# A graph layer and an attention layer in one kernel: row sums and rows of logits taken another way

## The chip, the cores and the metric

The kernel runs on one core of one Trainium2 chip. The metric is device time of one launch in microseconds (us). TensorE does the matmuls, VectorE (DVE) and ScalarE (ACT) read their results from PSUM, GpSimd (POOL) works on SBUF alone, and SyncE (SP) issues nearly all DMAs.

## The reference, cut to what matters

There are 64 samples of 256 tokens with 512 features, all in float32, and one adjacency matrix of 256 x 256 for all of them.

```python
h = relu(layernorm(x))                                    # layer 0
Wh = h @ W;  e_src = Wh @ a_src;  e_dst = Wh @ a_dst
logits = leaky_relu(e_src[:, :, None] + e_dst[:, None, :], 0.2)
attn = softmax(where(adj == 0, -inf, logits))             # over the last axis
x = x + attn @ Wh
h = relu(layernorm(x))                                    # layer 1: 8 heads of 64
q, k, v = heads of h @ Wq.T + bq, h @ Wk.T + bk, h @ Wv.T + bv
attn = softmax(where(adj == 0, -inf, q @ k.T / 8))
x = x + concat(attn @ v) @ Wo.T + bo
```

Two things in it matter here. In layer 0 a logit is the sum of a number of the row and a number of the column. And each softmax needs its row's sum, in layer 0 one for each of 256 rows, in layer 1 one for each of 8 x 256.

## The kernel before, in words

A group g is one sample; there are G = 64. Tokens or features lie on the 128 partitions. Each stage of the work on a group is a Python generator that gives out a piece at each `yield`, and the lists `first_half` and `second_half` (L1025 to L1031) say by hand in which order the pieces of different groups follow each other. The order in which instructions are given out is the order on each engine. Iteration i works on scores of group i, on layer 0 of groups i+1 to i+3, and on the output of groups before; the second member of each pair in the lists is what is added to i. Big products are done with seven block products in place of eight (`products`, matmuls at L207 and L216), whose sums are put together by VectorE (L192 to L203, `add_to_rows` at L701) and whose operands are prepared by GpSimd (`combine`, L165 to L168). PSUM is a ring of eight banks (`bank`).

The stages that the change touches:

- `normalize0` (D0 is its last piece, at i+2). It ends with es and ed, the numbers of the rows and columns, as scalar products of h with two weight vectors: four instructions on VectorE (L511). es lies on partitions, as [128, 2].
- `weights0` (E0, at i+2, three pieces). It brings es into a row on all partitions: two transposes on TensorE (L525) into a bank `pe`. From this ScalarE makes exp of the sum and exp of 0.2 times the sum (L532, L533, four instructions), VectorE takes the maximum of the two (L537), which is exp of the leaky logit, GpSimd multiplies by the mask (em, L540) and adds the two halves (esum, L542). The third piece sums over partitions: a matmul of `ones` with esum (L556) gives the sum of each row, in all partitions at once, and VectorE makes reciprocals of it, in a tile of 128 x 256 (L558, L559).
- `quarters0` (Q0, at i+2) multiplies em by that tile on GpSimd (L578) and forms differences for the block products (eq, L588). `aggregate0` (U0 at i+2, its last piece US at i+1) does the products (L606).
- `attention` (six pieces; A at i, and A_OLD at i-1 for the last two). The pieces are the scores with their exponentials (L838, L846), four times masks and sums of two heads (L851, L853), and the values (L863, L871) with `head_sums`: eight matmuls, each in a 32-column strip of the array, give the sums of all heads (psm, L878), and VectorE the reciprocals rc (L886). Each head's row of rc is then spread over 64 partitions into rb, with eight DMAs from SBUF to SBUF (L909). `scale` (AS) multiplies by rb (L936).
- `bias_rows` (BO) adds the output bias to x on GpSimd (L929), `project_v` is V, `project_qk` is K, `output` is O, and `transform0` is W.

In the loop, groups from `PLAIN` = 3 on take the way with block products in layer 0; groups 0 to 2 take a plain one. SP issues, in this order within an iteration: the x load for group i+3 (L225), two stores of output rows (L957), and the eight rb DMAs.

Of the kernel before, what the change touches and what calls it, by code (L numbers as in the profile page):

```python
# [9 lines left out]
F32 = mybir.dt.float32  # L10
# [6 lines left out]
P = 128  # L17
# [6 lines left out]
Q = 32  # L24
# [4 lines left out]
def kernel(  # L29
# [26 lines left out]
    nc = tc.nc  # L56
    B, N, D = x.shape
    NC = N // P
    DC = D // P
    NT = GB * NC  # L60
    TOK = NT * P
    G = B // GB
    DH = D // HEADS
# [5 lines left out]
    dram = ctx.enter_context(tc.tile_pool(name="dram", bufs=1, space=bass.MemoryType.DRAM))  # L69
# [10 lines left out]
    ident = const.tile([P, P], F32, tag="ident", name="ident")  # L80
    make_identity(nc, ident)
    ones = const.tile([P, P], F32, tag="ones", name="ones")
# [49 lines left out]
    def bounded():  # L132
        weights = ctx_b.enter_context(tc.tile_pool(name="weights", bufs=1))
        big = ctx_b.enter_context(tc.tile_pool(name="big", bufs=1))
        work = ctx_b.enter_context(tc.tile_pool(name="work", bufs=1))
# [3 lines left out]
        def bank(shape, name):  # L139
            return ps_mm.tile(shape, F32, tag="mm", name=name)  # L140
# [207 lines left out]
        pick = weights.tile([P, P], F32, tag="pick", name="pick")  # L348
# [10 lines left out]
        def constants():  # L359

            ok = weights.tile([P, 2 * DC + 5], F32, tag="ok", name="ok")
            rows = weights.tile([P, 2 * DC], F32, tag="rows", name="rows")
            gms = []
            for n in range(2):
                w_q = whole((wq_sb, wk_sb)[n])  # L370

                gm = work.tile([P, DC, DH], F32, tag="gram", name=f"gram_{n}", bufs=2)
                gms.append(gm)
                for pair in range(2):
                    pg = bank([P, 2, DH], f"pgram_{n}_{pair}")
                    for e in range(2):
                        for c in range(DC):
                            for r in range(2):
                                at = e * P + r * DH
                                wc = w_q[c // 2][pair][:, c % 2, at : at + DH]  # L380
                                nc.tensor.matmul(
                                    pg[r * DH : (r + 1) * DH, e, :], wc, wc,
                                    start=(c == 0), stop=(c == DC - 1),
                                )
                    yield
                    nc.vector.tensor_copy(gm[:, 2 * pair : 2 * pair + 2, :], pg)
                    yield
            for n, gm in enumerate(gms):
                pgs = [bank([P, DC, DH], f"pgram2_{n}_{r}") for r in range(2)]
                for e in range(DC):  # L390
                    for r in range(2):
                        half_p = slice(r * DH, (r + 1) * DH)
                        part = gm[half_p, e, :]
                        nc.tensor.matmul(pgs[r][half_p, e, :], part, part, start=True, stop=True)
                yield
                for e in range(DC):
                    for r in range(2):
                        half_p = slice(r * DH, (r + 1) * DH)
                        ab = work.tile([P, DH], F32, tag="gabs", name=f"gabs_{n}_{e}_{r}")
                        nc.scalar.activation(  # L400
                            ab[half_p], pgs[r][half_p, e, :], AF.Abs,
                            accum_out=rows[half_p, n * DC + e : n * DC + e + 1],
                        )
                yield
            for _ in range(10):
                yield
            sq = weights.tile([P, 4], F32, tag="sq", name="sq")
            for j, col in enumerate((cols["bq"], cols["bk"])):
                junk = work.tile([P, DC], F32, tag="e2", name=f"junk_c_{j}")
                nc.vector.scalar_tensor_tensor(  # L410
                    junk, col, 1.0, col, op0=ALU.mult, op1=ALU.mult, accum_out=sq[:, j : j + 1]
                )
            for _ in range(4):
                yield
            pq = bank([P, 2], "pq")
            nc.tensor.matmul(pq, ones, sq[:, 0:2], start=True, stop=True)
            yield
            nc.vector.tensor_scalar(
                ok[:, 2 * DC + 2 : 2 * DC + 4], pq, 1.0, None, op0=ALU.is_le
            )  # L420
            yield
            for j in range(2):
                junk = work.tile([P, D], F32, tag="e2", name=f"junk_w_{j}")
                nc.vector.scalar_tensor_tensor(
                    junk, wa[j], 1.0, wa[j], op0=ALU.mult, op1=ALU.mult, accum_out=sq[:, 2 + j : 3 + j]
                )
                yield
            nc.vector.tensor_scalar(ok[:, 0 : 2 * DC], rows, 1.0, None, op0=ALU.is_le)
            nc.vector.tensor_scalar(ok[:, 2 * DC : 2 * DC + 2], sq[:, 2:4], 1.95, None, op0=ALU.is_le)
            yield  # L430
            big_v = weights.tile([P, 1], F32, tag="big_v", name="big_v")
            nc.vector.tensor_reduce(big_v, svs, AX.X, ALU.add)
            nc.vector.tensor_scalar(
                ok[:, 2 * DC + 4 : 2 * DC + 5], big_v, 1.0e6, None, op0=ALU.is_le
            )
            okm = weights.tile([P, 1], F32, tag="okm", name="okm")
            nc.vector.tensor_reduce(okm, ok, AX.X, ALU.min)
            for _ in range(12):
                yield
            pk = bank([1, 1], "pok")  # L440
            nc.tensor.matmul(pk, okm, ones[:, 0:1], start=True, stop=True)
            nc.vector.tensor_scalar(flag, pk, P - 0.5, None, op0=ALU.is_lt)
            yield
            picks()
            yield

        class Stats:

# [32 lines left out]
        def normalize0(g):  # L481
# [26 lines left out]
            for t in range(NT):  # L508
                for dst, a in ((es, 0), (ed, 1)):
# [3 lines left out]
                        accum_out=dst[:, t : t + 1],  # L513
                    )
            nodes[g] = h, es, ed
            yield

        def weights0(g):

            h, es, ed = nodes[g]  # L520
            edl = small.tile([P, NT], F32, tag="edl", name=f"edl_{g}")
            nc.scalar.mul(edl, ed, NEG_SLOPE)
            pe = bank([P, TOK], f"pe_{g}")
            for t in range(NT):
                nc.tensor.transpose(  # L525
                    pe[:, t * P : (t + 1) * P], es[:, t : t + 1].to_broadcast([P, P]), ident
                )

            e1 = work.tile([P, NC, N], F32, tag="e1", name=f"e1_{g}")
            e2 = work.tile([P, NC, N], F32, tag="e2", name=f"e2_{g}")  # L530
# [10 lines left out]
            esum = work.tile([P, N], F32, tag="esum", name=f"esum_{g}")  # L541
            engine.tensor_tensor(esum, em[:, 0, :], em[:, 1, :], op=ALU.add)  # L542
            edges[g] = [em]
            yield

            if g == 0:
                ps = bank([P, NT], f"ps_{g}")
# [11 lines left out]
            nc.vector.reciprocal(rs, rs)  # L559
            edges[g].append(rs)  # L560
            yield


        PLAIN = 3

        def quarters0(g):

# [257 lines left out]
        def attention(g):  # L825
# [46 lines left out]

            def head_sums():

                psm = bank([P, N], f"psm_{g}")
                for r in range(2):
                    for e in range(DC):
                        nc.tensor.matmul(  # L878
                            psm[e * Q : (e + 1) * Q, :],
                            half[:, r, :],  # L880
                            sums[e][:, r, :],
                            start=(r == 0),
                            stop=(r == 1),
                        )
                rc = work.tile([P, N], F32, tag="rc", name=f"rc_{g}")
                nc.vector.reciprocal(rc, psm)  # L886
                return rc

            exs = [scores(e) for e in range(DC)]
# [13 lines left out]
                rc = head_sums()  # L903
            if g < G - 2:
                rb = work.tile([P, DC, N], F32, tag="rb", name=f"rb_{g}")
                for e in range(DC):
                    for r in range(2):
                        src = rc[e * Q + r * (Q // 2) : e * Q + r * (Q // 2) + 1, :]
                        nc.sync.dma_start(  # L909
                            rb[r * DH : (r + 1) * DH, e, :],  # L910
                            bass.AP(
                                tensor=src.tensor, offset=src.offset,
                                ap=[src.ap[0], [0, DH], [1, N]],
                            ),
                        )
            else:

                yield
                rb = [bank([P, N], f"prb_{g}_{e}") for e in range(DC)]
                for e in range(DC):  # L920
                    rows = slice(e * Q, (e + 1) * Q)
                    nc.tensor.matmul(rb[e], pick[rows, :], rc[rows, :], start=True, stop=True)
            outs[g] = aT, rb
            yield

# [89 lines left out]
        def aside(n=1):  # L1015
# [5 lines left out]
        Q0 = (quarters0, 2)  # L1021
# [1 line left out]
        A, A_OLD, BO = (attention, 0), (attention, -1), (bias_rows, 0)  # L1023
        AS, AS_OLD = (scale, -1), (scale, -2)
        first_half = [  # L1025
            (load, 3), O, D0, K, AS_OLD, O, K, O, K, E0, O, K, E0, O, US, A_OLD, K, O, K, BO, O, K, E0,
        ]
        second_half = [
            A_OLD, A, Q0, A, W, N0, W, W, V, N0, W, W, W, N1, W, N1, A, V, V, V, A, N0, N1, U0, V, AS,
            U0, X1, V, X1, V, X1,  # L1030
        ]  # L1031

# [259 lines left out]
```

## Time and profile before

| | |
|---|---|
| median of three runs | 2847.4 us (2846.96 to 2849.59) |
| the profiled execution | 2846.97 us |
| its span | 2845.2 us |
| TensorE busy | 2828.9 us (99%) |
| VectorE busy | 2473.5 us (87%) |
| GpSimd busy | 1607.0 us (56%) |
| ScalarE busy | 1257.3 us (44%) |
| TensorE clock granted | full, in the whole span |

A float32 matmul shows as two records, a transpose as one. Records of matmuls overlap, [...]so the distance between two starts says what a group costs, not its busy time. The time of an iteration is read from the distance of the same piece in two iterations. Names of tiles stand as out<-in; `pe`, `ps` and `psm` are the banks that are told of above.

### The profile page before, as it was taken

How to read it: one execution, taken by the hardware profiler on the slowest of the kernel's cores; microseconds unless marked ns; L12 is line 12 of the kernel's file. 1: busy time of each engine (PE TensorE's matmuls, PEld its weight loads, DVE VectorE, ACT ScalarE, POOL GpSimd, SP SyncE). 2: the span in 40 equal slices, each digit the busy share in tenths (PEclk: the TensorE clock that was granted, in tenths of full speed). 3: DMA queues.
4: the chain of work that ended last, by engine and by line, in shares of the span. 5: the costliest groups of instructions: out<-in, count | busy, mean ns of one | idle time of the engine just before them, and what ended most of it. 6: DMA issues, size and time to landing. Idle time of an engine off the chain costs nothing. (4 is left out here: it accounts for less than half of the span.)

```text
span 2845.2 us, 53317 instructions
## 1 busy us (share of the span) xinstructions
PE 2828.9 (99%) x20316; PEld 2472.3 (87%) x20316; DVE 2473.5 (87%) x3946; ACT 1257.3 (44%) x3045; POOL 1607.0 (56%) x2016
## 2 busy tenths in 40 slices
PE   9999999999999999999999999999999999999998
PEld 6888988988889889888898898888988988889886
DVE  7998988888889888888898888888988888889875
ACT  5444444443444444434444444344454443444532
POOL 2656556566565565665655655656556556565541
PEclk9999999999999999999999999999999999999999
DMA  4122122221221222212212222122122221221221
GB/s 134 23 38 38 34 42 33 36 45 31 38 38 34 42 33 36 45 31 38 39 33 42 33 36 46 31 38 40 32 42 33 36 45 31 38 42 30 34 42 27
DMA packets 82826, 111.01 MB, mean 39 GB/s; under 512 B 11524, under 2 KB 48644, under 8 KB 82566
## 3 DMA queue, kind: packets, MB, share of 16 engines
q1 hardware_dynamic: 82470, 107.53, 23.7%
q8 instruction: 164, 2.69, 0.4%
q14 instruction: 96, 0.79, 0.1%
q0 software_dynamic: 96, 0.01, 0.0%
HBM read 41.43 MB, written 33.55 MB: 26 GB/s over the span
## 5 line engine op out<-in xcount | busy, mean ns | idle before, releaser
L701 DVE TENSOR_TENSOR x<-po,x 128x1024 f32<-128x1024 f32 x875 | 593.8, 685 | 130.2 <-PE po L207 122.9
L851 DVE TENSOR_TENSOR ex<-ex,maskT 128x512 f32<-128x512 f32 x512 | 435.3, 890 | 0.0
L474 POOL TENSOR_SCALAR ve<-ssq 128x2 f32<-128x2 f32 x127 | 25.1, 198 | 483.8 <-ACT h L463 250.6
L846 ACT ACTIVATE ex<-psc 128x512 f32<-128x512 f32 x512 | 257.7, 627 | 89.5 <-PE psc L838 89.4
L871 ACT COPY aT<-pav 128x512 f32<-128x512 f32 x128 | 74.9, 585 | 499.2 <-PE pav L863 468.1
L511 DVE SCALAR_TENSOR_TENSOR junk<-wa,h 128x512 f32<-128x512 f32 x252 | 276.6, 1098 | 7.9 <-ACT h L504 1.1
L216 PEld LDWEIGHTS pqk<-hs,wq_sb 128*128 128x128 f32 x2016 | 264.4, 192 | 12.9
L216 PE MATMUL pqk<-hs,wk_sb 128*128 128x128 f32 x2016 | 266.3, 275 | 0.0
L216 PE MATMUL pqk<-hs,wq_sb 128*128 128x128 f32 x2016 | 265.8, 275 | 0.0
L207 PE MATMUL pv<-wv_sb,hs 128*128 128x256 f32 x1024 | 262.9, 380 | 0.6 <-DVE v L194 0.5
L540 POOL TENSOR_TENSOR em<-e,maskT 128x512 f32<-128x512 f32 x62 | 79.6, 1283 | 321.7 <-DVE e L537 312.0
L207 PE MATMUL po<-wo_sb,as 128*128 128x256 f32 x992 | 255.2, 380 | 0.0
L207 PE MATMUL po<-w_sb,us 128*128 128x256 f32 x1008 | 248.5, 379 | 0.0
L216 PEld LDWEIGHTS pqk<-hs,wk_sb 128*128 128x128 f32 x2016 | 245.4, 192 | 0.0
L838 PE MATMUL psc<-qk 64*128 64x256 f32 x2048 | 239.0, 383 | 0.3 <-DVE rc L886 0.3
L863 PE MATMUL pav<-ex,v 128*64 128x256 f32 x2048 | 235.4, 382 | 0.0
L838 PEld LDWEIGHTS psc<-qk 64*128 64x128 f32 x2048 | 193.1, 187 | 46.9 <-issue 25.0
L165 POOL TENSOR_TENSOR hs<-hT 128x256 f32<-128x256 f32 x64 | 47.0, 735 | 319.2 <-PE pv L207 319.2
L853 DVE TENSOR_TENSOR sm<-ex 128x512 f32<-128x512 f32 x256 | 210.5, 822 | 8.9
L863 PEld LDWEIGHTS pav<-ex,v 128*64 128x64 f32 x2048 | 141.2, 137 | 85.8 <-issue 20.3
L207 PEld LDWEIGHTS po<-w_sb,us 128*128 128x128 f32 x1008 | 191.4, 190 | 26.3 <-DVE x L701 0.3
L216 PEld LDWEIGHTS pqk<-hT,wq_sb 128*128 128x128 f32 x1512 | 198.2, 192 | 9.6
(211 smaller groups left out, 6564.5 us busy)
## 6 DMA issues: line engine op xcount, KB each, us to landing
x<-in_x_dram SPq DMA_DIRECT2D x64, 512.0 KB, 5.6
out_dram<-x SPq DMA_DIRECT2D x128, 256.0 KB, 2.0
rb<-rc SPq DMA_DIRECT2D x496, 64.0 KB, 4.9
wq_sb<-in_L_gnn_Wq_dram SPq DMA_DIRECT2D x4, 256.0 KB, 8.4
wk_sb<-in_L_gnn_Wk_dram SPq DMA_DIRECT2D x4, 256.0 KB, 6.7
w_sb<-in_L_gnn_W_dram SPq DMA_DIRECT2D x4, 256.0 KB, 6.6
wv_sb<-in_L_gnn_Wv_dram SPq DMA_DIRECT2D x4, 256.0 KB, 6.6
wo_sb<-in_L_gnn_Wo_dram SPq DMA_DIRECT2D x4, 256.0 KB, 6.0
```

What stands on the lines that cost most here:

```text
L165: nc.gpsimd.tensor_tensor(s[:, 0], a(1, 0), a(1, 1), op=ALU.add)
L207: nc.tensor.matmul(dst[:, 0:HD], left[:, c, :], wt[:, slot, c, :], start=c == 0, stop=c == 1)
L216: nc.tensor.matmul(dst[:, at : at + P], wt[:, slot, c, e * P : (e + 1) * P], left[:, c, :], start=c == 0, stop=c == 1,)
L511: nc.vector.scalar_tensor_tensor(junk, (wa if g else pas)[a], 1.0, h[:, t, :], op0=ALU.mult, op1=ALU.mult, accum_out=dst[:, t : t + 1],)
L540: engine.tensor_tensor(em, e1, maskT, op=ALU.mult)
L701: nc.vector.tensor_add(dst, src, dst)
L838: nc.tensor.matmul(psc[r][:, m, :], qk[rows, 2 + e % 2, m * P : (m + 1) * P], qk[rows, e % 2, :], start=True, stop=True,)
L846: nc.scalar.activation(ex[:, r, :, :], psc[r], AF.Exp, scale=SCALE)
L851: nc.vector.tensor_mul(ex[:, r, :, :], ex[:, r, :, :], maskT)
L853: nc.vector.tensor_add(sm, ex[:, :, 0, :], ex[:, :, 1, :])
L863: nc.tensor.matmul(pav[r * DH : (r + 1) * DH, i, :], v[j][:, m, at : at + DH], pair[i][:, r, m, :], start=(m == 0), stop=(m == NC - 1),)
L871: nc.scalar.copy(aT[j], pav)
```

## The change

For groups from 3 on:

1. es goes to DRAM as a row of 256 (one DMA), and comes back to all 128 partitions as `es_b` (a second DMA, in the buffer of esum). Both are issued at the end of `normalize0`. ScalarE reads `es_b` where it read the bank `pe`; the two transposes are gone.
2. The third piece of `weights0` is gone. In its place `head_sums` of group g sums the esum of group g+3 as well: four matmuls, each in a 32-column strip, each over 64 of the 256 columns, into 64 further columns of the psm bank. Maximum and reciprocal of these are on a tile of 128 x 64. The result goes to DRAM (one DMA) and comes back as `rb0` in all partitions (one DMA).
3. rc goes to DRAM in one DMA too, and rb comes back in two, in place of the eight.
4. In the order of the pieces, the first E0 stands later by one K and one O, the second E0 behind BO and A_OLD rather than ahead of US, the third is gone, and BO stands ahead of A_OLD. Near the end, one V stands ahead of both U0 rather than between them.

```diff
@@ normalize0
             nodes[g] = h, es, ed
+            if g >= PLAIN:
+                row_d = dram.tile([NT, P], F32, tag="row_d", name=f"row_d_{g}", bufs=2)
+                nc.sync.dma_start(row_d.rearrange("t p -> p t"), es)
+                es_b = work.tile([P, TOK], F32, tag="esum", name=f"es_b_{g}")
+                nc.sync.dma_start(
+                    es_b, bass.AP(tensor=row_d.tensor, offset=row_d.offset, ap=[[0, P], [1, TOK]])
+                )
+                nodes[g] = h, es_b, ed
             yield
@@ weights0
-            pe = bank([P, TOK], f"pe_{g}")
-            for t in range(NT):
-                nc.tensor.transpose(
-                    pe[:, t * P : (t + 1) * P], es[:, t : t + 1].to_broadcast([P, P]), ident
-                )
+            pe = es
+            if g < PLAIN:
+                pe = bank([P, TOK], f"pe_{g}")
...
             edges[g] = [em]
-            yield
+            if g >= PLAIN:
+                edges[g].append(esum)
+            yield
+            if g >= PLAIN:
+                return
@@ attention, head_sums
-                psm = bank([P, N], f"psm_{g}")
+                psm = bank([P, N + DH], f"psm_{g}")
+                rc = work.tile([P, N + DH], F32, tag="rc", name=f"rc_{g}")
+                g0 = g + PLAIN
+                if g0 < G:
+                    part = slice(N, N + DH)
+                    for e in range(DC):
+                        rows = slice(e * Q, (e + 1) * Q)
+                        nc.tensor.matmul(
+                            psm[rows, part], ones[:, 0:Q], edges[g0][1][:, e * DH : (e + 1) * DH],
+                            start=True, stop=True,
+                        )
...
-                rc = work.tile([P, N], F32, tag="rc", name=f"rc_{g}")
-                nc.vector.reciprocal(rc, psm)
+                if g0 < G:
+                    nc.vector.tensor_scalar_max(rc[:, part], psm[:, part], 1e-38)
+                    nc.vector.reciprocal(rc[:, part], rc[:, part])
+                    rows_d = dram.tile([P, DH], F32, tag="rows0_d", name=f"rows0_d_{g0}", bufs=2)
+                    nc.sync.dma_start(rows_d, rc[:, part])
+                    rb0 = work.tile([P, N], F32, tag="rb0", name=f"rb0_{g0}")
+                    nc.sync.dma_start(
+                        rb0.rearrange("p (e n) -> p e n", e=DC),
+                        bass.AP(
+                            tensor=rows_d.tensor, offset=rows_d.offset,
+                            ap=[[0, P], [Q * DH, DC], [1, DH]],
+                        ),
+                    )
+                    edges[g0][1] = rb0
+                nc.vector.reciprocal(rc[:, 0:N], psm[:, 0:N])
...
-                for e in range(DC):
-                    for r in range(2):
-                        src = rc[e * Q + r * (Q // 2) : e * Q + r * (Q // 2) + 1, :]
-                        nc.sync.dma_start(rb[r * DH : (r + 1) * DH, e, :], ...)
+                rows_d = dram.tile([P, N], F32, tag="rows_d", name=f"rows_d_{g}", bufs=2)
+                nc.sync.dma_start(rows_d, rc[:, 0:N])
+                for r in range(2):
+                    nc.sync.dma_start(
+                        rb[r * DH : (r + 1) * DH, :, :],
+                        bass.AP(
+                            tensor=rows_d.tensor, offset=rows_d.offset + r * (Q // 2) * N,
+                            ap=[[0, DH], [Q * N, DC], [1, N]],
+                        ),
+                    )
@@ the order
-            (load, 3), O, D0, K, AS_OLD, O, K, O, K, E0, O, K, E0, O, US, A_OLD, K, O, K, BO, O, K, E0,
+            (load, 3), O, D0, K, AS_OLD, O, K, O, K, O, K, E0, O, US, BO, A_OLD, K, E0, O, K, O, K,
...
-            A_OLD, A, Q0, A, W, N0, W, W, V, N0, W, W, W, N1, W, N1, A, V, V, V, A, N0, N1, U0, V, AS,
+            A_OLD, A, Q0, A, W, N0, W, W, V, N0, W, W, W, N1, W, N1, A, V, V, V, A, N0, N1, V, U0, AS,
             U0, X1, V, X1, V, X1,
```

A scratch tile of the checks at the start (`gabs`) moves into the buffer of rc, which is 64 columns wider.

More of the change, by code (lines that the diff above doesn't have):

```diff
@@ L398, in constants @@
                         half_p = slice(r * DH, (r + 1) * DH)
-                        ab = work.tile([P, DH], F32, tag="gabs", name=f"gabs_{n}_{e}_{r}")
+                        ab = work.tile([P, DH], F32, tag="rc", name=f"gabs_{n}_{e}_{r}")
                         nc.scalar.activation(
@@ L445, in constants @@
             yield
+        PLAIN = 3
         class Stats:
@@ L522, in weights0 @@
             nc.scalar.mul(edl, ed, NEG_SLOPE)
-            pe = bank([P, TOK], f"pe_{g}")
-            for t in range(NT):
-                nc.tensor.transpose(
-                    pe[:, t * P : (t + 1) * P], es[:, t : t + 1].to_broadcast([P, P]), ident
-                )
+            pe = es
+            if g < PLAIN:
+                pe = bank([P, TOK], f"pe_{g}")
+                for t in range(NT):
+                    nc.tensor.transpose(
+                        pe[:, t * P : (t + 1) * P], es[:, t : t + 1].to_broadcast([P, P]), ident
+                    )
             e1 = work.tile([P, NC, N], F32, tag="e1", name=f"e1_{g}")
@@ L561, in weights0 @@
             yield
-        PLAIN = 3
         def quarters0(g):
@@ L878, in head_sums @@
                         nc.tensor.matmul(
-                            psm[e * Q : (e + 1) * Q, :],
+                            psm[e * Q : (e + 1) * Q, 0:N],
                             half[:, r, :],
@@ L905, in attention @@
                 rb = work.tile([P, DC, N], F32, tag="rb", name=f"rb_{g}")
-                for e in range(DC):
-                    for r in range(2):
-                        src = rc[e * Q + r * (Q // 2) : e * Q + r * (Q // 2) + 1, :]
[L909 to L915, printed above, removed]
+                rows_d = dram.tile([P, N], F32, tag="rows_d", name=f"rows_d_{g}", bufs=2)
[7 more added lines that the diff above has]
+                        ),
+                    )
             else:
@@ L921, in attention @@
                     rows = slice(e * Q, (e + 1) * Q)
-                    nc.tensor.matmul(rb[e], pick[rows, :], rc[rows, :], start=True, stop=True)
+                    nc.tensor.matmul(rb[e], pick[rows, :], rc[rows, 0:N], start=True, stop=True)
             outs[g] = aT, rb
```

## The prediction

> **What bounds the kernel now.** I read the busy shares first, then one stretch of three samples, then TensorE's own order of time, then the waits, then the DMA issues. The page's head:
>
> ```profile
> span 2845.2 us, 53317 instructions
> PE 2828.9 (99%) x20316; PEld 2472.3 (87%) x20316; DVE 2473.5 (87%) x3946; ACT 1257.3 (44%) x3045; POOL 1607.0 (56%) x2016
> ```
>
> TensorE leaves 16 us free in the whole span. In the steady loop it leaves none: this is the table by stage (stretch, length, busy time of PE, PEld, DVE, ACT, POOL, clock, DMA share, GB/s).
>
> ```profile
> 1255.00:1386.25 131.25, 131.25 (x950) 115.76 (x949) 115.80 (x184) 58.41 (x142) 76.96 (x96) 1.00 0.24 37
> ```
>
> So one sample is 131.25 / 3 = 43.75 us of gapless TensorE work at full clock, and only two things can move the time: TensorE work taken out or put in, and a new wait of TensorE. The timeline of TensorE gives the price of what goes (start, busy time, line). First an iteration in the middle, then the one iteration near the end in which no layer 0 weights are made any more:
>
> ```profile
> 1393.65 1.06 PE L216 MATMUL pqk<-hT,wk_sb 128*128 128x128 f32 x8
> 1394.55 0.38 PE L525 MATMUL pe<-ident,es 128*128 128x128 f32 x2
> 1394.77 1.03 PE L207 MATMUL po<-wo_sb,as 128*128 128x256 f32 x4
> ...
> 1404.47 1.06 PE L216 MATMUL pqk<-hs,wk_sb 128*128 128x128 f32 x8
> 1405.37 0.60 PE L556 MATMUL ps<-esum,ones 128*128 128x256 f32 x2
> 1405.89 3.67 PE L863 MATMUL pav<-ex,v 128*64 128x256 f32 x32
> 1409.50 1.07 PE L878 MATMUL psm<-sm,half 128*32 128x256 f32 x16
> 1410.50 3.73 PE L838 MATMUL psc<-qk 64*128 64x256 f32 x32
> ```
>
> ```profile
> 2749.78 1.06 PE L216 MATMUL pqk<-hT,wk_sb 128*128 128x128 f32 x8
> 2750.67 1.03 PE L207 MATMUL po<-wo_sb,as 128*128 128x256 f32 x4
> ...
> 2760.38 1.06 PE L216 MATMUL pqk<-hs,wk_sb 128*128 128x128 f32 x8
> 2761.36 3.67 PE L863 MATMUL pav<-ex,v 128*64 128x256 f32 x32
> ```
>
> Busy times overlap, so I take differences of starts. The waits show that nobody holds TensorE up, while the other engines wait for it or for VectorE (who waited for whom, total us, times, longest):
>
> ```profile
> POOL em L540 <- DVE e L537: 312.0, 61, 7.7
> DVE rc L886 <- PE psm L878: 103.4, 63, 3.9
> PE pt L750 <- ACT xn L729: 4.9, 3, 3.1
> ```
>
> For the transfers that are added, the nearest rows (queue, count, KB, us from issue to landing), and for the added matmuls the nearest group, 64 columns wide in 64-column tiles (durations, first and last start):
>
> ```profile
> x<-in_x_dram SPq DMA_DIRECT2D x64, 512.0 KB, 5.6
> out_dram<-x SPq DMA_DIRECT2D x128, 256.0 KB, 2.0
> rb<-rc SPq DMA_DIRECT2D x496, 64.0 KB, 4.9
> bq_c<-in_L_gnn_bq_dram POOLq DMA_DIRECT2D x1, 2.0 KB, 5.7
> bk_c<-in_L_gnn_bk_dram POOLq DMA_DIRECT2D x1, 2.0 KB, 6.9
> ```
>
> ```profile
> L381 PE MATMUL pgram<-wq_sb x64: 222/222/270, 26.7 to 28.6; 128*64 128x64 f32 x64
> ```
>
> **What the Trainium skill says.** "TensorE: Matmul & The Clock Gate", Part 3, says that matmuls in different column groups of the array run at once. The trace agrees: the 16 psm records, in four column groups, take 1410.50 - 1409.50 = 1.00 us, where 16 records of 256 columns at the 0.216 us of an L207 record would take 3.46. "DMA: Bandwidth & Descriptors", Anatomy of one DMA, puts a fixed cost of about 2 us on a DMA, most of it the receipt of the write; the 2.0 us of the output stores agrees. Its Rules for kernel authors say that a last dimension that isn't contiguous becomes one descriptor per element, and that a DMA which reads what another wrote must wait for that one's semaphore before it is issued. The first bears on the write of es (256 elements of 4 bytes), the second makes each new trip two landings in series with SP waiting between. No steady transfer of before shows either.
>
> **The change, part by part, per sample (61 samples: 3 to 63).**
>
> *Two transposes of es (L525) go.* 1394.77 - 1393.65 = 1.12 us with them, 2750.67 - 2749.78 = 0.89 without: 0.22 us (1394.77 - 1394.55 says the same).
>
> *The sum over all rows (L556) goes.* 1405.89 - 1404.47 = 1.42 with it, 2761.36 - 2760.38 = 0.98 without: 0.44. The change of tile shape into pav (0.09) stays, so not the whole 0.52 is saved. Together 0.66 us of TensorE.
>
> *Four matmuls of 64 columns in 32-column tiles come (8 records).* pgram's 64 records take 1.9 / 63 = 30 ns each, two column groups at once. With four groups the 8 records are two rounds of four, about 60 ns a round, and a first round that is some 50 ns longer[...]: 0.12 to 0.17, and I take 0.15. Bounds: 0.11 (streaming alone: two rounds at half of the 0.111 us of an L216 record, which is 0.89 / 8 for 128 columns) and 0.50 (8 records at psm's mean of 1.00 / 16 = 62 ns). Net gain 0.66 - 0.15 = 0.51.
>
> *VectorE* loses a maximum (411 ns) and a reciprocal (1753 ns) over 256 columns and gets both over 64. Taken a quarter of the slope and the whole fixed part, about 0.21 and 0.55 us: 1.4 us less. VectorE is not the bound, so this is worth nothing by itself; it gives slack. The two stand ahead of the heads' reciprocal (L886) and after the new matmuls, so at worst L886 ends 0.76 us later. Waiting for it is the eighth bank of the next scores: before, L886 ends at 1412.4 and that bank is used at about 1410.50 + 2.8 = 1413.3. It fits, with 0.1 us to spare if the maximum has to wait for all of psm, and 0.8 if it starts as soon as the four small matmuls end.
>
> *es by way of DRAM.* VectorE ends es at 1394.4 (last L511). Write: between 2.0 (a store) and 6.9 (4-byte loads in the crowded start), taken 2.7. Read of 128 KB to all partitions: between 2.0 and 5.6, taken 2.9 (2 fixed plus a quarter of x's other 3.6). With issues 5.7 us: es_b at about 1400.1. Four exponentials take 1.9 us, to 1402.0. Behind them on ScalarE stand only the four p5 activations (1400.27 before, now to 1403.2), whose reader comes at about 1403.9. VectorE, which now does the masks of the last head pair (L851 and L853, 3.6 us) ahead of the maximum of e (L537), reaches that maximum at about 1402.5 (1394.4, then seven reads of O and K products in 4.5, then the masks), so it doesn't wait. GpSimd has meanwhile done the us sums and the bias rows, which are moved ahead. Then maximum 0.68, em 1.27, esum 1.05, with handovers 3.2: esum at 1405.7. The new matmuls need it at 1409.50 - 0.66 = 1408.8. Cover left: 3.1 us; VectorE, without L558 and L559 (2.2 us) and with its 1.58 of idle time ahead of L886, has some 3 likewise. So the maximum may start at 1405.6, es_b may land at 1403.7, and the trip may take 9.3 us before TensorE waits.
>
> *The reciprocals by way of DRAM.* Written from about 1410.1 (1411.0 in the late case): write 2.0 to 2.5, read in 512 pieces of 256 bytes about 3.5: rb0 at 1415.8 to 1416.8, where it used to lie ready. GpSimd's em by rb (L578) stands at 1411.28 before and waits now, some 5 us; behind it are the eq differences (3.0) and the closing of both norms (1419.78 and 1424.08). It ends eq at 1420.2 to 1421.2. The first use by TensorE is near 1424.1, as U0 is moved behind one more V product (0.87 us). The closing of the first norm is read by ScalarE only at 1423.89, that of the second keeps its place. Cover left: 2 to 3 us.
>
> *rb in 3 DMAs in place of 8.* SP's issues took 7 us from 1412.42; now the queue waits for three landings in series, write at 1413, rb at about 1422. Its reader (L936) comes at 1385.54 + 43.75 = 1429.3. The next x load, behind it on SP, is issued near 1418 (1419.43 before) and isn't needed for an iteration. Stores stand ahead of it. Nothing.
>
> *Swap of V and U0:* one V product's bank is released about 0.15 us before its next use, others get more room: 0 to 0.2 us of wait, taken 0.
>
> Sum: 61 x 0.51 = 31 us. The profiled execution took 2846.97 us (span 2845.2, 1.8 around it), 0.4 under the median of 2847.4: 2846.97 - 31 = **2816 us**.
>
> **Rivals.**
> *Thin covers or dearer small matmuls (0.20).* The 8 records at 62 ns make the net gain 0.16 (2837 us); a wait of 0.2 on a bank makes it 0.31 (2828). For it: 0.1 and 0.15 us of slack at two places. Against: four psm records start together in each round, and the bank slack was computed with the later of two starts.
> *The es trip is too long (0.10): slower.* If the 4-byte write costs what bq_c's load did, 5.7, and the read what rb's did, 4.9, with 0.2 between, es_b lands at 1405.2. The exponentials end at 1407.1, esum at 1410.3, and TensorE waits 1.5 us ahead of the new matmuls, every sample: 61 x (1.5 - 0.51) = +60, 2907 us. It decides from a trip of 9.3 + 0.5 = 9.8 us. Against: those two rows were taken in the crowded start and in a row of eight issues; this trip has the queue for itself.
> *The reciprocals' trip stalls GpSimd too long (0.06).* At 10.8 us as well, rb0 lands at 1421, the first norm's closing slips behind 1423.89, then xn and the transposes by some 2 us: 61 x 1.5 = +91, 2938 us. It has more room, and no 4-byte pieces.
> *Nothing happens (0.02):* TensorE's time isn't freed since something else bounds. The gapless stretch speaks against it.
>
> **How the numbers follow.** The forecast has 0.62, its own range 2812 to 2820 (0.12 to 0.17, and the whole 0.11 bound, 0.55 x 61 = 34). The rivals have 0.20, 0.10, 0.06, 0.02. For 8 in 10 I take the first rival in: 2811 to 2838. A measurement tells 0.2% (5.7 us) from no change; only a small part of the first rival and the last lie within it. Faster 0.81, same 0.03, slower 0.16.
>
> **What would show it.** L525 in three samples alone; 61 times 8 records of 64 columns before psm, 0.15 us from their first start to psm's; a period of 43.24 us; TensorE still busy for the whole of a steady stretch; es_b and rb0 as ends of waits on ScalarE and GpSimd (several us a sample) but not on TensorE; DVE busy near 2390. Wrong, if TensorE waits for esum or for the heads' reciprocal, or if the small matmuls run one by one.

## The result and the profile after

The changed kernel takes 3249.9 us (median of four runs, 3246.92 to 3253.66) where the kernel before takes 2848.07: a ratio of 1.1411, with a 95% interval of 1.1391 to 1.1431. It is 14% slower. 2816 us had been forecast, with 2811 to 2838 as the range.

The page's head of the changed kernel:

```profile
span 3251.0 us, 53678 instructions
PE 2913.3 (90%) x20560; PEld 2539.9 (78%) x20560; DVE 2374.8 (73%) x3946; ACT 1256.6 (39%) x3045; POOL 1588.1 (49%) x2016
```

TensorE, which had 16 us free, has 338 free now, though it has less to do; and it is busy for longer (2913 in place of 2829). The table by stage of one iteration says where (stretch, length, busy time of PE, PEld, DVE, ACT, POOL, clock, DMA share, GB/s):

```profile
1587.00:1609.00 22.00, 20.17 (x158) 17.98 (x157) 14.26 (x23) 5.14 (x15) 13.09 (x15) 1.00 0.07 19
1609.00:1628.30 19.30, 18.67 (x132) 16.28 (x132) 17.40 (x28) 9.98 (x25) 8.64 (x13) 1.00 0.20 54
1628.30:1637.20 8.90, 5.25 (x23) 4.40 (x22) 4.58 (x12) 4.38 (x7) 2.14 (x6) 0.81 0.20 67
1637.20:1650.00 12.80, 12.80 (x100) 12.34 (x99) 10.95 (x18) 1.35 (x5) 11.95 (x14) 1.00 0.02 1
```

There are two holes, one before 1609 and a large one behind 1628.3, and over the third stretch, which holds the large one, the mean granted clock is down to 0.81. The same iteration in TensorE's timeline (start, busy time, line; in brackets the idle time before and who ended it):

```profile
1603.50 3.67 PE L879 MATMUL pav<-ex,v 128*64 128x256 f32 x32
1609.08 0.32 PE L899 MATMUL psm<-esum,ones 128*32 128x64 f32 x8 [1.90 <-POOL esum L556]
1609.21 1.05 PE L905 MATMUL psm<-sm,half 128*32 128x256 f32 x16
...
1627.87 0.61 PE L622 MATMUL pu<-em,hq 128*128 128x128 f32 x4
1632.14 1.12 PE L766 MATMUL pt<-ident,xn 128*128 128x128 f32 x4 [3.65 <-ACT uT L633]
1633.05 1.92 PE L207 MATMUL pv<-wv_sb,hT 128*128 128x256 f32 x4
```

The small matmuls wait for esum, and the transposes of layer 1 wait for a bank that ScalarE's copy of uT sets free. Behind that wait a group of four V records takes 1.70 us (1633.05 to 1634.75), where it took 0.87 before: the clock granted in those 1.70 us was 0.50. The waits over the whole span (who for whom, total us, times, longest):

```profile
ACT e L546 <- DMA es_b<-row_d: 743.5, 61, 12.9
POOL em L594 <- DMA rb<-rows_d: 574.2, 61, 12.7
...
ACT h L507 <- POOL nmr L479: 231.0, 59, 5.7
...
PE pt L766 <- ACT uT L633: 170.8, 58, 3.7
...
PE psm L899 <- POOL esum L556: 122.3, 61, 3.4
...
PE pu L622 <- POOL eq L604: 22.6, 29, 1.7
```

Both new trips by way of DRAM end in waits. The transfers (queue, count, KB, us from issue to landing):

```profile
es_b<-row_d SPq DMA_DIRECT2D x61, 128.0 KB, 4.8
rb<-rows_d SPq DMA_DIRECT2D x61, 128.0 KB, 8.1
rows_d<-rc SPq DMA_DIRECT2D x61, 32.0 KB, 1.4
...
row_d<-es SPq DMA_DIRECT2D x61, 1.0 KB, 8.5
```

The smallest of these transfers, 1 KB of es, takes the longest: 8.5 us. It doesn't stand in a queue of data: in this iteration it is issued at 1641.69 and the read that waits for it at 1649.79, and in the stretch from 1637.20 to 1650.00 the DMA engines are busy for a share of 0.02. The read of rb0 takes 8.1 (its row is `rb<-rows_d` with 128.0 KB). How the second gets from the DMA to TensorE is seen on GpSimd and then on ScalarE:

```profile
1611.61 0.73 POOL L168 TENSOR_TENSOR hq<-h,hq 128x256 f32<-128x256 f32 x1
1622.68 1.86 POOL L594 TENSOR_TENSOR em<-em,rb 128x256 f32<-128x256 f32 x2 [10.33 <-DMA rb<-rows_d]
...
1627.29 0.52 POOL L477 TENSOR_SCALAR ve<-ssq 128x2 f32<-128x2 f32 x1
...
1628.67 0.20 POOL L479 TENSOR_TENSOR nmr<-nmean,rstd 128x2 f32<-128x2 f32 x1
```

```profile
1628.90 1.52 ACT L507 ACTIVATE h<-x,nmr,rstd 128x512 f32<-128x512 f32 x2 [5.09 <-POOL nmr L479]
1630.33 1.50 ACT L745 ACTIVATE xn<-x,nmr,rstd 128x512 f32<-128x512 f32 x2
1631.73 0.35 ACT L633 COPY uT<-pu 128x256 f32<-128x256 f32 x1
```

GpSimd stands for 10.33 us at the multiplication by rb0. Behind it, in its queue, is the closing of the first norm (L477 to L479). ScalarE waits 5.09 us for that, does two norms, and only then copies the first product of U0 out of its bank, which the transposes need.

### The profile page after: what moved, and what is told of

The parts are those of the page before. It is cut to its first block, busy times and chain, and to the rows that moved or that the text cites. A ratio compares the mean times of both kernels' runs of the same rounds, so it can differ in the third digit from the quotient of the medians.

```text
span 3251.0 us, 53678 instructions
## 1 busy us (share of the span) xinstructions
PE 2913.3 (90%) x20560; PEld 2539.9 (78%) x20560; DVE 2374.8 (73%) x3946; ACT 1256.6 (39%) x3045; POOL 1588.1 (49%) x2016
## 5 line engine op out<-in xcount | busy, mean ns | idle before, releaser
L867 DVE TENSOR_TENSOR ex<-ex,maskT 128x512 f32<-128x512 f32 x512 | 400.4, 822 | 0.5 <-ACT ex L862 0.2
L594 POOL TENSOR_TENSOR em<-em,rb 128x256 f32<-128x256 f32 x122 | 107.7, 903 | 574.2 <-DMA rb<-rows_d 574.2
L546 ACT ACTIVATE e<-es_b,ed 128x256 f32<-128x256 f32 x122 | 61.0, 500 | 743.5 <-DMA es_b<-row_d 743.5
L551 DVE TENSOR_TENSOR e<-e,e 128x512 f32<-128x512 f32 x64 | 44.3, 693 | 370.6 <-ACT e L547 370.6
L514 DVE SCALAR_TENSOR_TENSOR junk<-wa,h 128x512 f32<-128x512 f32 x252 | 259.9, 1031 | 7.9 <-ACT h L507 1.1
L854 PE MATMUL psc<-qk 64*128 64x256 f32 x2048 | 257.7, 404 | 6.0 <-DVE qk L201 3.0
L766 PE MATMUL pt<-ident,xn 128*128 128x128 f32 x512 | 104.0, 339 | 175.8 <-ACT uT L633 170.8
L854 PEld LDWEIGHTS psc<-qk 64*128 64x128 f32 x2048 | 226.8, 200 | 43.8 <-issue 35.7
L766 PEld LDWEIGHTS pt<-ident,xn 128*128 128x128 f32 x512 | 77.6, 175 | 201.0 <-ACT uT L633 181.8
L207 PE MATMUL pv<-wv_sb,hT 128*128 128x256 f32 x768 | 226.5, 423 | 0.0
## 6 DMA issues: line engine op xcount, KB each, us to landing
rows_d<-rc SPq DMA_DIRECT2D x62, 128.0 KB, 7.9
es_b<-row_d SPq DMA_DIRECT2D x61, 128.0 KB, 4.8
rb<-rows_d SPq DMA_DIRECT2D x61, 128.0 KB, 8.1
```

The lines of the kernel that those rows point to most:

```text
L207: nc.tensor.matmul(dst[:, 0:HD], left[:, c, :], wt[:, slot, c, :], start=c == 0, stop=c == 1)
L514: nc.vector.scalar_tensor_tensor(junk, (wa if g else pas)[a], 1.0, h[:, t, :], op0=ALU.mult, op1=ALU.mult, accum_out=dst[:, t : t + 1],)
L546: nc.scalar.activation(e1[:, m, :], pe, AF.Exp, bias=ed[:, m : m + 1])
L594: nc.gpsimd.tensor_tensor(em[:, m, :], em[:, m, :], rb, op=ALU.mult)
L766: nc.tensor.transpose(pt[:, c, :], xn[:, t, c * P : (c + 1) * P], ident)
L854: nc.tensor.matmul(psc[r][:, m, :], qk[rows, 2 + e % 2, m * P : (m + 1) * P], qk[rows, e % 2, :], start=True, stop=True,)
```

## The experiments

All were run beside the kernel before, at 2847.0 to 2847.7 us.

**One trip taken away.** `no es trip`: the DMAs of es are left out, and the transposes are back.

```diff
-            if g >= PLAIN:
-                row_d = dram.tile([NT, P], F32, tag="row_d", name=f"row_d_{g}", bufs=2)
-                nc.sync.dma_start(row_d.rearrange("t p -> p t"), es)
...
-            pe = es
-            if g < PLAIN:
+            if True:
                 pe = bank([P, TOK], f"pe_{g}")
```

> The changed kernel with es brought into a row by the two transposes again (no trip of es by way of DRAM); all else as changed. Theory (each of the two trips costs a stall of its own): in the changed kernel TensorE waits some 1.9 us ahead of the new small matmuls for esum, and some 3.8 us ahead of the transposes of layer 1 (plus about 2 us at a reduced clock and at eq) for the late rb0. Without the es trip the first wait goes and the second stays, since rb0 still lands about 11 us after the small matmuls: 3250 - 61 x (1.9 - 0.2) = about 3145 us. Rival one (the es trip starts the whole chain): about 2830 us. Rival two (the trip of the reciprocals alone sets the time): about 3250 us.

Measured: 3050.25 us, 1.0711 of the kernel before (1.0689 to 1.0732). The wait for esum is gone, that for the transposes stays:

```profile
PE pt L756 <- ACT uT L623: 132.3, 46, 3.6
```

So neither rival holds: each trip has its own wait. The size was missed by 95 us, for two reasons that the traces show. The first: in 15 of the 61 iterations, every fourth, rb0 comes quickly. A read of it issued at 903.97 is used by GpSimd at 908.70, the next one, issued at 947.40, at 955.37. In such an iteration TensorE doesn't wait at the transposes, and it takes 43.4 us where the others take some 48; the forecast had the stall in every one. The pieces are as many and as large as in the slow reads, and why they come faster isn't shown. The second: the two trips are not independent. In the changed kernel VectorE is behind after its late maximum of e, and takes up the small sums 1.94 us after the small matmuls start; without the es trip it does so after 1.25. So a late es makes rb0 later still, by 0.7 us.

**rb0 read in large pieces.** Each strip of psm holds the same 64 sums in all its rows, so one partition of each will do:

```diff
-                    rows_d = dram.tile([P, DH], F32, tag="rows0_d", ...)
-                    nc.sync.dma_start(rows_d, rc[:, part])
+                    rows_d = dram.tile([DC, DH], F32, tag="rows0_d", ...)
+                    nc.sync.dma_start(rows_d, rc[0:P:Q, part])
                     nc.sync.dma_start(
-                        rb0.rearrange("p (e n) -> p e n", e=DC),
-                        bass.AP(..., ap=[[0, P], [Q * DH, DC], [1, DH]]),
+                        rb0,
+                        bass.AP(..., ap=[[0, P], [1, N]]),
                     )
```

> The changed kernel with the layer 0 reciprocals written to DRAM as one row of 256 (four rows of 64 taken from one partition of each strip), so that rb0 is read in 128 pieces of 1 KB in place of 512 pieces of 256 bytes; the same 128 KB. Theory (pieces): the read took 8.1 us as 512 packets came 15.5 ns apart; with 128 it lands in 3 to 3.5 us, the wait ahead of the transposes goes, that for esum stays: 2816 + 61 x 1.9 = about 2930 us, between 2890 and 2950. Rival (bytes out of one spot of DRAM): still about 8 us, about 3250 us. Rival (the queue of SP and what stands in it): still about 8 us, about 3250 us.

Measured: 2926.7 us, 1.0277 of the kernel before (1.0256 to 1.0297). The transfers and waits of this kernel:

```profile
rb<-rows_d SPq DMA_DIRECT2D x61, 128.0 KB, 3.1
...
row_d<-es SPq DMA_DIRECT2D x61, 1.0 KB, 7.9
```

```profile
PE psm L899 <- POOL esum L556: 93.1, 61, 2.5
```

The same 128 KB, copies of the same 256 numbers, land in 3.1 us as 128 pieces and in 8.1 as 512. The wait of the transposes is gone, that for esum is left. Both rivals would have left 8 us, and the size came as the theory of pieces had it. The edit changes the place too, though: the 512 pieces come from four rows that lie 8 KB apart, the 128 from one row of 1 KB.

**es written in pairs.** The two numbers of a partition go to DRAM side by side, and ScalarE reads the row with a step of two:

```diff
-                row_d = dram.tile([NT, P], F32, tag="row_d", ...)
-                nc.sync.dma_start(row_d.rearrange("t p -> p t"), es)
+                row_d = dram.tile([P, NT], F32, tag="row_d", ...)
+                nc.sync.dma_start(row_d, es)
...
-            pe = es
+            pe = es.rearrange("q (p t) -> q t p", t=NT) if g >= PLAIN else es
```

> The changed kernel with es written to DRAM as it lies (128 pieces of 8 bytes in place of 256 of 4), and read by ScalarE with a step of two elements; the same bytes. Theory (pieces): the packets of the write are done 0.25 us after the first, but it lands only 8 us after its issue, 27 ns for each of 256 small writes; with 128 it lands in about 4.5 us, and the wait for esum ahead of the small matmuls goes: 3250 - 61 x 1.9 = about 3134 us. Rival (a fixed cost of any such small write, or the queue): still about 8 us, 3250 us. A side cost would be exponentials slower than 0.50 us through the step of two.

Measured: 3103.31 us, 1.0897 of the kernel before (1.0875 to 1.0919). The write:

```profile
row_d<-es SPq DMA_DIRECT2D x61, 1.0 KB, 2.9
```

It falls from 8.5 to 2.9 us, more than half, which a cost for each piece doesn't give; the wait for esum is gone, and the exponentials take 527 ns with the step of two, 500 without. The time is still 53 us above the run that had no es trip at all, though that one has the transposes to do. By an estimate a large part of this is the number of quick reads of rb0: 3 iterations of 61 here, 15 there, at some 4.8 us each.

**Both trips mended.** The last two edits together.

> The two edits of the runs before together: es in 128 pairs, reciprocals as one row. Theory (both covers hold again as the prediction had them): the es trip some 8 us, rb0 at 5 us after the small matmuls, no wait of TensorE left: 2816 to 2830 us, faster than before by 0.6 to 1.1%. Rival (the es trip is still longer than its cover of 9.3 us, or another wait comes): 2850 to 2900 us.

Measured: 2820.29 us (2817.78 to 2821.29, four runs), 0.9903 of the kernel before (0.9886 to 0.9919): this version beats both. Its page and a stretch of three samples:

```profile
span 2817.5 us, 53678 instructions
PE 2799.5 (99%) x20560; PEld 2454.3 (87%) x20560; DVE 2332.7 (83%) x3946; ACT 1264.8 (45%) x3045; POOL 1484.7 (53%) x2016
```

```profile
1255.00:1384.60 129.60, 129.60 (x962) 114.72 (x961) 108.80 (x184) 58.73 (x141) 70.85 (x97) 1.00 0.19 47
```

TensorE is without a gap again. Its timeline around the small matmuls, and GpSimd's around rb0:

```profile
1438.63 3.67 PE L882 MATMUL pav<-ex,v 128*64 128x256 f32 x32
1442.23 0.32 PE L902 MATMUL psm<-esum,ones 128*32 128x64 f32 x8
1442.37 1.05 PE L908 MATMUL psm<-sm,half 128*32 128x256 f32 x16
```

```profile
1405.73 1.42 POOL L597 TENSOR_TENSOR em<-em,rb 128x256 f32<-128x256 f32 x2 [7.30 <-DMA rb<-rows_d]
...
1409.43 0.19 POOL L477 TENSOR_SCALAR ve<-ssq 128x2 f32<-128x2 f32 x1 [0.50 <-ACT h L466]
```

The eight small records cost 0.14 us (1442.23 to 1442.37). GpSimd still waits 7.30 us at rb0, and then 0.50 more for ScalarE ahead of the closing: the stall no longer delays the closing, with half a microsecond to spare, and ScalarE starts on its result only at 1413.54, 2.9 us after it is there (1410.68). With these four kernels the losses stand in a square (us):

| | rb0 in 512 pieces | rb0 in 128 pieces |
|---|---|---|
| es in 256 pieces of 4 bytes | 3249.9 | 2926.7 |
| es in 128 pieces of 8 bytes | 3103.3 | 2820.3 |

The slow es alone costs 106, the slow rb0 alone 283, the two together 430, 40 more than their sum.

**Number or place of the small pieces.** With es in pairs and rb0 slow, es lies with gaps in SBUF, so that its pieces have 4 bytes again and their places in DRAM are those of the pairs:

```diff
-            es = small.tile([P, NT], F32, tag="es", name=f"es_{g}")
+            es = small.tile([P, NT, 2], F32, tag="es", name=f"es_{g}")[:, :, 0]
```

> The kernel with es in pairs (third run), but with the two columns of es kept apart in SBUF, so that its write is 256 pieces of 4 bytes again, now to the DRAM order of the pairs (neighbouring pieces of one partition are neighbours in DRAM). The reciprocals' trip as in the changed kernel. If the number or size of the pieces made the write slow: it takes some 8 us again and the time is near that of the changed kernel, 3220 to 3250 us. If the place of the pieces in DRAM did (two far halves, written by turns): about 3 us, and 3103 us as with pairs.

Measured: 3114.88 us, and the write

```profile
row_d<-es SPq DMA_DIRECT2D x61, 1.0 KB, 7.0
```

So the pieces make it slow, not where they lie; the place is worth 0.9 to 1.5 us (7.0 here, 7.9 and 8.5 in the two kernels with the halves apart). The time rose by 12 us alone, where 117 to 147 had been expected: against the changed kernel's 13.6 us, this trip takes 11.2 from issue to the first exponential (7.03 to the issue of the read and 4.18 more), which the cover nearly holds: TensorE waits for esum 6 times, for 4.6 us in all.

**Number or size.** Two kernels, whose logits in layer 0 are not the reference's, set these apart. In the first every es is written with a zero beside it, 256 pieces of 8 bytes; in the second only one column is written, 128 pieces of 4.

```diff
+            es_w = small.tile([P, NT, 4], F32, tag="es", name=f"es_{g}")
+            nc.gpsimd.memset(es_w, 0.0)
+            es = es_w[:, :, 0]
...
-                row_d = dram.tile([P, NT], F32, tag="row_d", ...)
-                nc.sync.dma_start(row_d, es)
+                row_d = dram.tile([P, NT, 2], F32, tag="row_d", ...)
+                nc.sync.dma_start(row_d, es_w[:, :, 0:2])
```

> What makes the write of es slow, the number of its pieces or their size. The kernel with es in pairs (third run, slow rb0), where each value of es is written together with a zero: 256 pieces of 8 bytes, 2 KB in all, in place of 128 of 8 or 256 of 4. es_b is read from the first half of it, so the logits of layer 0 are not the reference's; a clearing of es on GpSimd (some 0.1 us) is added. The time from the write's issue to the read's issue was 2.95 us with 128 pieces of 8 bytes and 7.0 with 256 of 4. If the number decides: 7 us or more and about 3115 us. If the size does: 3 to 3.5 us and about 3105 us.

```diff
-                row_d = dram.tile([NT, P], F32, tag="row_d", ...)
-                nc.sync.dma_start(row_d.rearrange("t p -> p t"), es)
+                row_d = dram.tile([P, 1], F32, tag="row_d", ...)
+                nc.sync.dma_start(row_d, es[:, 0:1])
                 nc.sync.dma_start(
-                    es_b, bass.AP(..., ap=[[0, P], [1, TOK]])
+                    es_b.rearrange("p (t n) -> p t n", t=NT),
+                    bass.AP(..., ap=[[0, P], [0, NT], [1, P]]),
                 )
```

> The other side of the same question: the changed kernel, where only the first of the two columns of es is written, 128 pieces of 4 bytes, and read twice (256 pieces of 512 bytes), so the second half of the row of logits is not the reference's. If the number of pieces decides, the write takes about what 128 pieces of 8 bytes did, 3 us; if their size does, well over that, about half of the 8.6 us of 256 such pieces or more, 4.5 to 7 us. The read, in 256 pieces at 15 ns, takes some 5 us.

Measured: 3078.31 and 3113.99 us, one execution each. The writes, first of the kernel with 256 pieces of 8 bytes, then of that with 128 of 4, whose read of es_b stands above it:

```profile
row_d<-es SPq DMA_DIRECT2D x61, 2.0 KB, 3.5
```

```profile
es_b<-row_d SPq DMA_DIRECT2D x61, 128.0 KB, 6.1
...
row_d<-es SPq DMA_DIRECT2D x61, 0.5 KB, 7.2
```

The size decides. Twice the pieces of 8 bytes cost 0.6 us more (3.5 against 2.9); half the pieces of 4 bytes cost no less than all of them in the same order (7.2 against 7.0). These rows are medians of the transfers whose landing the trace could place; from the issue of the write to that of the read, over all 61, it is 3.6 against 2.95, and 7.3 against 7.0. The theory of the third run, 27 ns for each small write, is wrong. Why a piece of 4 bytes is so much dearer than one of 8 isn't shown by these runs. As every number here is a float32, they don't tell a size of 4 bytes from a single number in a piece, either. In the second kernel the read of es_b is 256 pieces of 512 bytes out of one place and lands in 6.1 us, between the 128 and the 512 pieces seen so far. Its trip is as long as the changed kernel's (13.5 us to the first exponential), yet TensorE waits for esum for only 4.7 us in the whole span: the write needs one column alone, and is issued at 1523.04, while the second column is ready at 1525.28. That the first kernel is 25 us below the one with 128 pairs goes with a quicker rb0 (11.5 us after the small matmuls, in place of 12.1), whose cause isn't shown.

**The place in GpSimd's queue.** With es in pairs and rb0 as slow as ever, the multiplication by rb0 is moved behind the closing of the first norm:

```diff
                 combine(a, s)
+                yield
                 for m in range(NC):
                     nc.gpsimd.tensor_tensor(em[:, m, :], em[:, m, :], rb, op=ALU.mult)
...
-            A_OLD, A, Q0, A, W, N0, W, W, V, N0, W, ...
+            A_OLD, A, Q0, A, W, N0, W, W, V, N0, Q1, W, ...
```

> The kernel with es in pairs and the slow rb0 (third run), with one edit in the order of GpSimd's work: the multiplications by rb0 and the differences behind them stand after the closing of the first norm (second N0), not ahead of it; the sums of h stay where they were. The DMA is as slow as before. Theory (rb0 costs so much since the closing of the norms stands behind it on GpSimd, and ScalarE, the bank of the first product and the transposes behind that): the first closing is on time, the second is 1 to 1.5 us late, so most of the wait goes: 2880 to 2930 us. Rival (the products themselves wait for rb0, wherever the multiplication stands): 3103 us as before.

Measured: 2977.49 us, 126 below the kernel without the move, at the same DMA. TensorE's waits of this kernel:

```profile
PE pt L770 <- ACT uT L637: 110.3, 61, 2.2
...
PE pu L626 <- POOL eq L608: 11.4, 27, 1.5
```

The products hardly wait for rb0 itself (11.4 us in the whole span). The wait ahead of the transposes falls from 174.4 us (57 waits, in the third run) to 110.3. It stays longer than expected since the second norm's closing is now late: in one iteration it ends at 1541.41, 3.9 us behind the 1537.53 at which ScalarE had the sums for it, and ScalarE waits 2.50 us. So what stood behind the wait in GpSimd's queue made up 126 of the 283 us that the slow rb0 costs, and the second norm, which still stands there, holds part of the rest. Part of the 126 came by way of the clock: with waits of at most 2.2 us at the transposes, in place of 3.7, its mean over the span is 0.990, in place of 0.969.

**rb in eight DMAs as before**, with both trips mended (the hunk of the change on rb undone).

> The kernel with both trips mended (fourth run), with rb spread by the eight DMAs of the kernel before in place of three by way of DRAM. Theory (this part of the change lies under seven us of cover and costs and brings nothing): 2820 us, within 0.2%. Rival (the eight issues hold SP for 7 us, and what stands behind them, the x load and the write of es, comes late): above 2830 us.

Measured: 2818.48 us (2817.4 to 2819.54), 0.9898 of the kernel before (0.9882 to 0.9915), the same as the 2820.29 with three DMAs. That part of the change neither costs nor brings anything.

**The sums alone**, with transposes of es and the mended rb0 (edits of the first two runs together).

> The kernel with es brought into a row by transposes, and the sums of layer 0 beside the heads' sums with the reciprocals' trip mended: the second part of the change alone, in the changed order. Theory: TensorE saves 0.44 and pays 0.14 us a sample, 0.30 x 61 = 18: 2829 us, 0.6% under the kernel before. The transposes are then worth the 0.22 x 61 = 13 us between this and the fourth run's 2820 (within some us). Rival (another wait stays): above 2847 us.

Measured: 2831.47 us, 0.9946 (0.993 to 0.9963). 16 us come from the sums (18 had been forecast), and 11 more from the transposes (13).

## Why the prediction was wrong

**TensorE's own work: right.** 0.66 us a sample were to go and 0.15 to come, for a period of 43.24 us. The small matmuls cost 0.136 (median of 61), and once no trip stalls, the period is 43.2 (2820.29 us where 2816 had been forecast from this sum). Nothing in the arithmetic of TensorE was off by more than the 4 us between these two. The late case of the maximum of the small sums came true (it starts 1.25 us after the small matmuls, behind all of psm), and fitted as computed. The three DMAs for rb, with the x load behind them, cost nothing, as said; the swap of V and U0 was not run alone, but 2820.29 us leaves it no more than a few us.

Two terms of the sum failed, the durations of the two trips; the waits that were set at nothing rested on them.

**The first term that failed: "es by way of DRAM".** The write was put between 2.0 and 6.9 us and taken as 2.7; it took 8.5. The read was taken as 2.9; it took 4.8, and 3.8 in the mended kernel. The upper bound was no bound: it came from loads of 4-byte pieces out of DRAM, issued by GpSimd in the start, which say nothing of writing such pieces into it, and the value taken lay next to the row of stores in pieces of 2 KB. Nor does a fixed part of 2 us show: that was the landing of a store of 256 KB, and in the changed kernel a write of 32 KB lands in 1.4. The sum for the cover was nearly right: 9.3 us from the end of the scalar products, which is 10.4 from the issue, as es is complete one instruction (1.1 us) ahead of ed. With a trip of 12.65 us (the second run, 7.99 and 4.66) that gives a wait of 2.25; TensorE waited 93.1 / 61 = 1.53, so the cover was some 0.7 us longer, and a trip of 11.2 us just fitted. Alone, this term makes the kernel slower than before: 106 / 61 = 1.74 us a sample are lost, and 0.5 gained. The rival "the es trip is too long" named place and chain rightly, with a chance of 0.10 that rested on the same rows.

**The second, and the dearer: the read of rb0.** "512 pieces of 256 bytes about 3.5" measured 8.1. It had an upper end nowhere in the text; its rival borrowed 10.8 us from the other trip. em by rb0 was forecast 7 to 8 us after the small matmuls, came after 12.6, and after 6.8 in the mended kernel. Alone, it costs 283 us, of the 430 that both cost.

**What a late rb0 costs: mechanism right, size too small.** The rival named the closing of the first norm behind L578 on GpSimd, then xn and the transposes, at some 2 us a sample (1.5 net of the gain). It had rb0 at 1421, 12 us after the small matmuls, which is about when it came; but it costs 283 / 61 = 4.6. ScalarE does the norms of two stages before the copy of uT, so the bank comes later than xn; and a reduced clock after the hole was in no sum. Of the 433 us between the spans of the changed and the mended kernel, 2913.3 - 2799.5 = 114 are longer busy time of TensorE for the same work, the rest idle time. The mean clock of 0.970 accounts for some 97 of the 114 at most (0.030 x 3251).

**The combination.** The two slower rivals were priced as alternatives, 0.10 and 0.06, each with the other trip in order. Both came at once, and the first fed the second: with es in pairs em is multiplied by rb0 12.1 us after the small matmuls, with the late es 12.6.

## What to carry to other kernels

A trip by way of DRAM in place of a little TensorE work is paid in latency, and its latency has to be taken from a transfer with the same piece size in the same direction; where there is none, measure the trip alone before anything else is built on it. Choose the layout in DRAM so that both the write and the read have large pieces, and let the reading engine put up with a stride. Before a wait is put on an engine with its work in order, ask what stands behind it there: here a wait at one multiplication delayed two norms that had nothing to do with it.

## What the runs showed of the hardware that had not been expected

- Writes to DRAM in pieces of 4 bytes land late, 128 of them as late as 256: 7.2 us for 128, 7.0 to 8.5 for 256, against 2.9 for 128 and 3.5 for 256 pieces of 8 bytes, and 1.4 for 128 pieces of 256 bytes. In the trace of the changed kernel the packets of one such write, 256 of 4 bytes, lie within 0.25 us, at 1642.6 to 1642.8; the read behind it is issued at 1649.79. So the time passes behind the last packet.
- A small place in DRAM read to all partitions, 128 KB in all, took longer in more pieces: 8.1 us in 512 of 256 bytes, 6.1 in 256 of 512 bytes, 3.1 (rb0) to 4.8 (es_b) in 128 of 1 KB. In the trace of the changed kernel the 512 packets of one rb0 start about 15.5 ns apart in the mean, over 7.9 us. The number is not the whole of it: without the es trip every fourth read of rb0, with the same 512 pieces, was in use 4.7 us after its issue, where the next took 8.0. What makes the difference stays open.
- After a hole of 3.65 us, 1628.49 to 1632.14, TensorE's clock was granted at 0.50 up to 1634.75, and at 1.00 again from 1635.44; the 0.81 of the table is the mean over hole and all. Shorter waits cost less of it: the mean over the span is 0.970 in the changed kernel, 0.990 where the waits at the transposes are at most 2.2 us, and 0.997 where only the waits for esum are left, of at most 2.5 us.
